# Moments and scaling of the second sequence's tiles beside value matmuls, and softmax totals spread through DRAM instead of through the array

## The chip, the core and the metric

The kernel runs on one core of one Trainium2 chip. The metric is the device time of one execution in microseconds; lower is better. Besides the times there is one profiled execution, whose trace holds every engine's instructions with their begin and end.

## What is computed

The input is `x` with 4 sequences of 1024 rows and 1024 columns, all in fp32. First comes attention, then a top-1 mixture of small adapters, each with a residual:

```python
x = x + attn(layernorm(x), wq, wk, wv, wo)     # 32 heads of 32, rotary q and k, causal softmax
x = x + ffn(layernorm(x), route_w, A, Bw)      # 8 experts of rank 16, the best one by logit
# attn: probs = softmax(scores); out = probs @ v; out @ wo
```

The softmax is computed without its division: exponentials go into the value product, and the product is then multiplied by the reciprocals of the rows' totals.

## The kernel before, in words

**Tiling.** Four heads fill 128 partitions, so a sequence has 8 groups and the program has 32 *units* `(b, g)`, numbered `u` = 0 to 31. A unit projects q, k and v of the next unit (six chains of eight 128x128x512 matmuls, lines 337 and 385), computes its own scores (L430) round by round, and multiplies exponentials by values (L626). The 1024 queries of a unit are two *blocks* of 512; block 1 of unit `u` is finished early in unit `u+1`.

**Order.** All instructions are written out in one order; each engine runs its own in that order, and semaphores join them. `SLOTS` lists the eleven rounds of a unit: score rounds, with "second" (apply block 1 of the unit before) and "first" (apply block 0 of this unit) among them. Between rounds, `fill` takes *steps* from a queue `todo`: projections of the next unit, and from the second sequence on also the output projection (L743) and the adapter stage (L765, L804) of a tile of the sequence before, whose weights are streamed as chunks (L700). `postponed` holds small pieces of work that are let go after so many steps' cost.

**One round.** The scores land in the one PSUM tile `s` (pool `ps_s`, one buffer). ACT copies them to `pr` (L441), POOL adds the causal mask (L444), DVE finds each row's maximum (L462, L483), ACT takes exponentials and their row sums (L491), DVE transposes them in 32x32 squares (L516). `apply` then runs the value matmuls in two pieces, into the same PSUM tile `s`; between the pieces it calls `meanwhile`, which transposes the next values (L1087). `scale_values` (L646, two DVE instructions of 128x256) multiplies the product by the totals' reciprocals `by`, and only then is the PSUM tile free for the next score round.

**The reciprocals.** `join_sums` adds the row sums (L559) and takes the reciprocal (L560) as soon as a block's transposes are out. The reciprocals stand one per query row, and `by` needs them along the free axis, repeated over the 32 rows of each head. There are two ways:

- *By turning* (before: all of the first sequence, 16 blocks). POOL spreads them to `by` (L563); `spread_sums` transposes `by` with four 128x128 matmuls against the identity (L597), and ACT copies the result back (L598).
- *By DRAM* (before: the other three sequences, 48 blocks). DVE transposes them (L570, `recT`); `put` writes them to DRAM in four transfers (L576), `get` reads them back with each row repeated over 32 partitions, in four transfers (L581). All eight are issued by SP, whose queue also carries every other transfer of the kernel, in the written order. `put` waits for `recT`, `get` for `put` to land.

**The next sequence's input.** Class `Norm` holds it. `load` fetches a 128-row tile of `x`; `find` computes mean and variance on DVE (two L178, then L180, L182) and the reciprocal root on POOL (L184); `scale` applies them on DVE (L189); `turn` transposes the tile on the array. For the second sequence, tiles 0 to 5 are loaded, found and scaled by steps put into the queue of units 1, 2, 3, 4 and twice 5; tiles 6 and 7 have their own places in unit 6 (`own` steps), and the turning is done in units 6 and 7.

Of the kernel before, what the change touches and what calls it, by code (L numbers as in the profile page):

```python
# [71 lines left out]
def tile_preln_attn_then_top1_lora(  # L72
# [24 lines left out]
    NG = HEADS // HG  # L97
# [112 lines left out]
    units = [(b, g) for b in range(B) for g in range(NG)]  # L210
# [335 lines left out]

    bys = {}

    def join_sums(u, blk):

        if (u, blk) in bys or any((u, t) in places for t in range(blk * QT, (blk + 1) * QT)):
            return
        den = dens.pop((u, blk)).rearrange("p (t c) h -> p c h t", c=2)
        rec = rec_sb[:, blk, : HG * TB].rearrange("p (h t) -> p h t", t=TB)
        for i in range(P // SQ):
            rows, other = slice(i * SQ, (i + 1) * SQ), slice((i ^ 1) * SQ, ((i ^ 1) + 1) * SQ)
            nc.vector.tensor_tensor(rec[rows], den[rows, i % 2], den[other, i % 2], ALU.add)  # L559
        nc.vector.reciprocal(rec_sb[:, blk, : HG * TB], rec_sb[:, blk, : HG * TB])  # L560
        if units[u][0] == 0:
            by = big.tile([P, TB, P], F32, tag="by", name=f"by_{u}_{blk}")
            nc.gpsimd.tensor_copy(  # L563
                by.rearrange("p t (h d) -> p t h d", d=HD),
                rec.rearrange("p h t -> p t h").unsqueeze(3).to_broadcast([P, TB, HG, HD]),
            )
            bys[u, blk] = by, None
            return
        turned = small.tile([P, SQ], F32, tag="recT", name=f"recT_{u}_{blk}", bufs=2)
        nc.vector.transpose(turned, rec_sb[:, blk])  # L570
        there = dram.tile([HG * TB, P // SQ, SQ], F32, tag="recs", name=f"recs_{u}_{blk}")
        by = big.tile([P, TB * P], F32, tag="by", name=f"by_{u}_{blk}")

        def put():
            for i in range(P // SQ):
                nc.sync.dma_start(there[:, i], turned[i * SQ : i * SQ + HG * TB])  # L576

        def get():
            for h in range(HG):
                of_h = there[h * TB : (h + 1) * TB]  # L580
                nc.sync.dma_start(  # L581
                    by[h * HD : (h + 1) * HD],
                    bass.AP(of_h.tensor, of_h.offset, [[0, HD], [1, TB * P]]),
                )

        left = [put, get]
        bys[u, blk] = by, left
        for cost in (2.0, 5.0):
            postponed.append([cost, lambda: left and left.pop(0)()])
# [279 lines left out]
    def behind(steps, at, step):  # L869

        steps.insert(steps.index(at) + 1, step)

    norms = {}
    between, late_fetch = [], {}
    tail = []
    for u, (b, g) in enumerate(units):
        project, new_tail = [], []
        if b:
            fetch, (project,), new_tail = finish_steps(
                b - 1, g, "resident" if u == len(units) - 1 else "stream"  # L880
            )
            if g:
                apart = 3 if g + 1 == NG and u + 1 < len(units) else 8
                between[-1].insert(max(0, len(between[-1]) - apart), fetch)
            else:
                late_fetch[u] = fetch

        if u + 1 < len(units) and g + 1 == NG:  # L890
            last_v = between[-1]
            if b:
                norm = Norm(b + 1, {0: (2,), 2: (5,), 3: (6,)}, {3: "q", 4: "k", 6: "q"})
                load = [Step(lambda norm=norm, t=t: norm.load(t), 0.0) for t in range(2)]
                for at, step in (
                    (own["k", 0][0], load[0]),
                    (own["v", 0][0], norm.finding(0)),
                    (own["v", 0][1], load[1]),
                    (own["v", 0][2], norm.scaling(0)),
                    (own["v", 0][4], norm.finding(1)),  # L900
                    (own["v", 0][6], norm.turning(0)),
                    (own["v", 0][7], norm.scaling(1)),
                    (own["k", 1][2], norm.finding(2)),
                    (own["k", 1][3], norm.turning(1)),
                    (own["k", 1][5], norm.scaling(2)),
                ):
                    behind(last_v, at, step)
            else:

                norm = Norm(b + 1, {0: (7,)}, {5: "chunk", 6: "chunk"})  # L910
                for t, (unit, at) in enumerate(((1, 24), (2, 24), (3, 24), (4, 24), (5, 12), (5, 36))):
                    steps = between[unit]
                    for k, step in enumerate((norm.load, norm.find, norm.scale)):
                        steps.insert(at - 8 + 5 * k, Step(lambda step=step, t=t: step(t), 0.0))
                for at, step in (
                    (own["q", 0][0], Step(lambda norm=norm: norm.load(6), 0.0)),
                    (own["q", 1][0], norm.finding(6)),
                    (own["q", 1][3], norm.scaling(6)),
                    (own["v", 1][5], norm.finding(7)),
                    (own["v", 1][7], norm.scaling(7)),  # L920
                ):
                    behind(last_v, at, step)
                for t, at in enumerate((("k", 1), ("k", 1), ("k", 1), ("v", 1))):
                    behind(last_v, own[at][(1 + 3 * t) % NC], norm.turning(t))
            steps = change_steps(u + 1, norm, project, tail, held)
            norms[b + 1] = norm
        else:
            steps = []
            held = []
            if u + 1 < len(units):  # L930


                ends = g + 2 == NG and b + 1 < B
                own = {}
                for n, tb in ENDING if ends else USUAL:
                    own[n, tb] = chain(u + 1, n, tb)
                    if ends and b and (n, tb) == ("v", 1):
                        held = own[n, tb]
                    else:
                        steps += own[n, tb]  # L940
            if not steps:
                steps = list(project)
            elif b and not g:
                steps = steps[:36] + weave(steps[36:], project)
            else:
                steps = weave(steps[:-6], project) + steps[-6:]
            if u + 1 == len(units):
                new_tail6 = tail
            n = len(steps)
            for k, s in reversed(list(enumerate(tail))):  # L950
                steps.insert(6 + k * n // 7, s)
        between.append(steps)
        tail = new_tail
# [110 lines left out]
    second, first_ = SLOTS.index("second"), SLOTS.index("first")  # L1064
    final = len(units) - 1
    for u, (b, g) in enumerate(units):
# [10 lines left out]
        for r, pieces in enumerate(SLOTS):  # L1077
            if pieces == "second":
                release_exps()
            if pieces == "second":  # L1080
# [4 lines left out]

                def meanwhile():
                    nc.vector.transpose(vTs[u], vTs[u])  # L1087

                if u:
                    apply(u - 1, 1, meanwhile)  # L1090
# [3 lines left out]
            elif pieces == "first":  # L1094
                apply(u, 0)
                find_tops(u)
                ended.clear()
            else:
                release_exps()
                turn_probabilities()  # L1100
                if second < r < first_:
                    join_sums(u, 0)
                score_round(u, pieces)
                if r == second - 1 and u:
                    while any((u - 1, t) in places for t in range(QT, 2 * QT)):
                        exponentiate_some(1)
                        turn_probabilities()
                    join_sums(u - 1, 1)
                if r != first_ - 1:
                    find_tops(u)  # L1110
                exponentiate_some(SHARE / 3)
                next_exp.extend((u, t, h) for t in ended for h in range(HG))
                if r != first_ - 1:
                    ended.clear()
                if r in (second + 1, first_ + 1):
                    for put in stores:
                        put()
                    stores.clear()
                    if u == final and r == first_ + 1:
                        load_adapter()  # L1120
                if r == second + 2:
                    scatter(loads, 2)
                    if u in late_fetch:
                        do(late_fetch[u])
                        for k in range(3 if b == 1 else 0):
                            load_chunk(k)
# [75 lines left out]
```

## Time and profile before

| what | value |
|---|---|
| time, median of 3 runs | 2752.6 us (2751.11 to 2756.06) |
| profiled execution: its own time | 2752.48 us |
| its span, first to last instruction | 2750.7 us |
| mean granted TensorE clock | 0.992 |
| a unit of the first sequence, V transpose to V transpose (L1087), units 1 to 5 | 68.3 to 72.1 us |
| a steady unit of the second sequence | 81.5 us |
| L597 four transposes of `by`: PE MATMUL x64 | 287 ns each by the record |
| L598 copy of `by` on ACT x16; L563 spread on POOL x16 | 581 ns; 612 ns |
| L570 `recT` on DVE x48 | 211 ns |
| L576, L581 issue on SP, x192 each | median 412 ns, 419 ns |
| L178 moments, L189 scaling of a tile (DVE) | 682 ns each of two; 1043 ns |

In the profile, PE is TensorE's matmuls, PEld its weight loads, DVE VectorE, ACT ScalarE, POOL GpSimd, SP the queue that issues transfers (SPq its instruction stream). A timeline row has its begin and length in us, the engine, the line, the operation, the tiles written and read, and how many alike follow each other; in brackets stands the idle time of the engine just ahead and what released it. One fp32 matmul stands in the records as two passes, so a chain of eight steps is 16 records.

### The profile page before, as it was taken

To read this page: it belongs to the slowest core of one execution; us is meant where nothing else is said; L and a number is where in the kernel's file an instruction comes from. 1 tells how busy PE (TensorE), PEld (TensorE's weight loads), DVE (VectorE), ACT (ScalarE), POOL (GpSimd) and SP (SyncE) were. 2 spreads that over 40 slices of the span, in tenths; PEclk is the share of its full clock that TensorE was granted. 3 is DMA by queue.
4 is the path that set the end of the run, shared out by engine and by line. 5 is a ranking of instruction groups with operands and counts; after the bars stand their busy time and mean duration, and the time that the engine had idled before them with its cause. 6 is when DMAs were issued, how large, how long until landed. Compare 5 with 4: busy or idle time off the path is not lost.

```text
span 2750.7 us, 84042 instructions
## 1 busy us (share of the span) xinstructions
PE 2680.1 (97%) x35136; PEld 1307.2 (48%) x35136; DVE 2143.1 (78%) x4249; ACT 1727.5 (63%) x4985; POOL 608.5 (22%) x852
## 2 busy tenths in 40 slices
PE   8999999999999999989999999998999999999998
PEld 5444444444445444444444454444544444444445
DVE  4888889887877877887777778787777777788555
ACT  2877777776666766666666666665576665666521
POOL 2222222222222222212222222221222221222000
PEclk9999999999999999999999999999999999999999
DMA  3222222225544455661655544565255555446421
GB/s 117 52 63 63 63 71 71 63 48 126 154 131 130 136 154 143 157 181 51 182 139 141 134 125 125 154 177 148 66 167 153 139 140 135 126 126 203 133 71 54
DMA packets 463659, 330.84 MB, mean 120 GB/s; under 512 B 159536, under 2 KB 380976, under 8 KB 463280
## 3 DMA queue, kind: packets, MB, share of 16 engines
q1 hardware_dynamic: 463280, 325.47, 43.5%
q8 instruction: 276, 4.52, 0.7%
q14 instruction: 103, 0.84, 0.1%
HBM read 275.17 MB, written 50.20 MB: 118 GB/s over the span
## 4 chain that ended last, share of the span: by engine, by line
PE 79%; DVE 13%; ACT 2%; DMA 2%; POOL 1%; issue 1%; SPq 1%; POOLq 0%; DVEq 0%; ACTq 0%
PE po L743 14%; PE pq L337 14%; PE pk L337 13%; PE pv L337 12%; PE s L430 11%; PE av L626 8%; DVE pr L516 4%; DVE top L462 4%; PE ph L765 2%; PE pf L804 2%; DMA chunk<-in_wo 1%; ACT pr L441 1%; DVE both L483 1%; PE pt_f L201 1%; ACT pr L491 1%
## 5 line engine op out<-in xcount | busy, mean ns | idle before, releaser
L491 ACT ACTIVATE pr<-pr,both 128x256 f32<-128x256 f32 (+15 forms) x2048 | 1044.5, 518 | 68.8 <-DVE both L483 68.8
L441 ACT COPY pr<-s 128x640 f32<-128x640 f32 (+14 forms) x544 | 525.3, 1017 | 678.8 <-PE s L430 678.1
L462 DVE TENSOR_REDUCE top<-pr 128x2 f32<-128x960 f32 (+15 forms) x768 | 650.8, 894 | 267.3 <-POOL pr L444 266.7
L516 DVE STREAM_TRANSPOSE pr<-pr 128x1024 f32<-128x1024 f32 (+11 forms) x768 | 664.4, 907 | 35.1 <-ACT pr L491 31.7
L444 POOL TENSOR_TENSOR pr<-pr,causal_sb 128x128 f32<-128x128 f32 x512 | 240.8, 477 | 1173.7 <-ACT pr L441 1165.4
L337 PE MATMUL pv<-xnT,wv 128*128 128x512 f32 x1024 | 488.7, 604 | 0.0
L337 PE MATMUL pq<-xnT,wq 128*128 128x512 f32 x1008 | 479.3, 603 | 0.2 <-ACT xnT L203 0.2
L337 PE MATMUL pk<-xnT,wk 128*128 128x512 f32 x1008 | 476.4, 602 | 0.0
L430 PE MATMUL s<-kT,qT 32*32 32x256 f32 (+4 forms) x17408 | 398.5, 390 | 21.1 <-DVE at L646 13.4
L491 ACT ACTIVATION_READ_ACCUMULATOR pr<-pr,both 128x1 f32 x2048 | 400.4, 195 | 0.0
L743 PE MATMUL po<-chunk,attn 128*128 128x512 f32 x736 | 383.7, 607 | 9.0 <-DMA chunk<-in_wo 8.6
L430 PEld LDWEIGHTS s<-kT,qT 32*32 32x32 f32 x17408 | 189.4, 103 | 280.4 <-issue 123.2
L337 PEld LDWEIGHTS pk<-xnT,wk 128*128 128x128 f32 x1008 | 181.2, 190 | 234.7 <-issue 234.3
L337 PEld LDWEIGHTS pv<-xnT,wv 128*128 128x128 f32 x1024 | 187.1, 191 | 220.2 <-issue 219.6
L337 PEld LDWEIGHTS pq<-xnT,wq 128*128 128x128 f32 x1008 | 183.9, 192 | 226.6 <-issue 224.8
L626 PE MATMUL av<-pr,vals 64*32 64x256 f32 (+3 forms) x12288 | 271.7, 319 | 7.4 <-DVE pr L516 6.8
L626 PEld LDWEIGHTS av<-pr,vals 64*32 64x32 f32 x12288 | 213.1, 106 | 116.6 <-issue 68.9
L483 DVE TENSOR_TENSOR both<-top 32x4 f32<-32x4 f32 (+3 forms) x1152 | 204.9, 178 | 23.8
L743 PEld LDWEIGHTS po<-chunk,attn 128*128 128x128 f32 x736 | 135.7, 191 | 178.0 <-issue 144.7
L646 DVE TENSOR_TENSOR at<-av,by 128x256 f32<-128x256 f32 x128 | 48.1, 417 | 123.6 <-PE av L626 79.6
L743 PE MATMUL po<-wo,attn 128*128 128x512 f32 x256 | 117.7, 601 | 0.0
L375 POOL TENSOR_TENSOR qT<-qT,swapq 128x512 f32<-128x512 f32 x64 | 81.7, 1277 | 146.3 <-DVE swapq L371 146.3
(89 smaller groups left out, 1575.7 us busy)
## 6 DMA issues: line engine op xcount, KB each, us to landing
chunk<-in_wo SPq DMA_DIRECT2D x368, 256.0 KB, 4.0
vals<-vd SPq DMA_DIRECT2D x256, 128.0 KB, 4.4
x<-in_x SPq DMA_DIRECT2D x56, 512.0 KB, 5.4
wq<-in_wq SPq DMA_DIRECT2D x32, 512.0 KB, 4.7
wk<-in_wk SPq DMA_DIRECT2D x32, 512.0 KB, 4.0
wv<-in_wv SPq DMA_DIRECT2D x32, 512.0 KB, 4.4
vd<-vT SPq DMA_DIRECT2D x128, 128.0 KB, 4.8
out_y<-x SPq DMA_DIRECT2D x32, 512.0 KB, 2.6
```

The lines of the kernel that those rows point to most:

```text
L337: nc.tensor.matmul(at["p"], lhsT=wt[:, c, :], rhs=xnTs[b, tb][:, c, :], start=(c == 0), stop=(c == NC - 1),)
L375: nc.gpsimd.tensor_tensor(dst[:, cols], dst[:, cols], other, ALU.add)
L430: nc.tensor.matmul(sc[i * SQ : (i + 1) * SQ, h, at : at + w].rearrange("p (j k) -> p j k", k=SQ), lhsT=of_q[rows, 2 * t + half], rhs=of_k[ ...
L441: nc.scalar.copy(pr[:, :, k0 : k0 + w], sc[:, :, at : at + w])
L444: nc.gpsimd.tensor_tensor(diagonal, diagonal, causal_sb.unsqueeze(1).to_broadcast([P, HG, SQ]), ALU.add)
L462: nc.vector.tensor_reduce(top[:, k, h : h + step], places[u, t][:, h : h + step, :], AX.X, ALU.max, negate=True,)
L483: nc.vector.tensor_tensor(dst[rows], src[rows], src[other], op)
L491: nc.scalar.activation(pr[:, h, :], pr[:, h, :], AF.Exp, bias=tops[u, t][:, h : h + 1], accum_out=dens[u, t // QT][:, t % QT, h : h + 1],)
L516: nc.vector.transpose(pr, pr)
L626: nc.tensor.matmul(avs[half][h * HD : (h + 1) * HD, t0:, :], lhsT=v[rows, j, h * HD : (h + 1) * HD], rhs=rhs, start=(j == 0), stop=(j == n ...
L743: nc.tensor.matmul(st["po"], lhsT=lhsT, rhs=rhs, start=(c == start), stop=(c == stop))
L765: nc.tensor.matmul(ph, lhsT=st["ynT"][:, c, :], rhs=w[:, c - i * RA, :], start=(c == 0), stop=(c == NC - 1),)
```

## The change

It has two parts. First, in the first sequence the totals go by DRAM too, and the turning is kept for blocks near a change of sequence: with `at = u + blk`, those with `at` 0, with `at % 8 == 7`, with `at` 32, and block 0 of unit 6. So 12 blocks of the first sequence (block 1 of units 0 to 5 and 7, block 0 of units 1 to 5) change from turning to DRAM, and 7 blocks of later sequences ((14,1), (15,0), (22,1), (23,0), (30,1), (31,0), (31,1)) change from DRAM to turning.

Second, tiles 0 to 5 of the second sequence are loaded by a step at the end of units 0 to 5; their moments are found in `meanwhile` of the following unit (between the two pieces of value matmuls of "second", behind the V transpose), and their scaling is put ahead of the score round that follows "second". Of the instructions that each engine is given, the order changes as follows. DVE has the moments between L1087 and L646 of block 1, and the scaling behind the transposes that follow L646, ahead of that round's maxima; before, both stood between the rounds of tiles 15 and 14. In unit 6 tile 5's and tile 6's moments and scalings both stand ahead of that L646. POOL has L184 ahead of the qT addition of L375 in place of behind it. SP has the eight transfers of a block just ahead of the store of that block's product (L659).

```diff
+    def by_turning(u, blk):
+        at = u + blk
+        return at == 0 or at % NG == NG - 1 or at >= len(units) or (u, blk) == (NG - 2, 0)
...
-        if units[u][0] == 0:
+        if by_turning(u, blk):
...
-                for t, (unit, at) in enumerate(((1, 24), (2, 24), (3, 24), (4, 24), (5, 12), (5, 36))):
-                    steps = between[unit]
-                    for k, step in enumerate((norm.load, norm.find, norm.scale)):
-                        steps.insert(at - 8 + 5 * k, Step(lambda step=step, t=t: step(t), 0.0))
+                for t in range(NG - 2):
+                    ahead_of[t + 1] = (
+                        lambda norm=norm, t=t: norm.find(t),
+                        lambda norm=norm, t=t: norm.scale(t),
+                    )
+                    between[t].append(Step(lambda norm=norm, t=t: norm.load(t), 0.0))
...
                 def meanwhile():
                     nc.vector.transpose(vTs[u], vTs[u])
+                    if u in ahead_of:
+                        ahead_of[u][0]()
...
                     join_sums(u, 0)
+                if r == second + 1 and u in ahead_of:
+                    ahead_of[u][1]()
                 score_round(u, pieces)
```

More of the change, by code (lines that the diff above doesn't have):

```diff
@@ L871, in behind @@
         steps.insert(steps.index(at) + 1, step)
-    norms = {}
+    norms, ahead_of = {}, {}
     between, late_fetch = [], {}
```

## The prediction, as put on record

> **What bounds the kernel now.** I read the page first: busy shares, then the chain that ended last.
>
> ```profile
> PE 2680.1 (97%) x35136; PEld 1307.2 (48%) x35136; DVE 2143.1 (78%) x4249; ACT 1727.5 (63%) x4985; POOL 608.5 (22%) x852
> PE 79%; DVE 13%; ACT 2%; DMA 2%; POOL 1%; issue 1%; SPq 1%; POOLq 0%; DVEq 0%; ACTq 0%
> ```
>
> PE bounds the whole, but DVE holds 13% of the chain. Where? The windows view, by stage (per engine: busy us and count; then the granted clock, DMA share and GB/s):
>
> ```profile
> 142.10:493.20 351.10, 332.54 (x5180) 157.06 (x5188) 302.49 (x592) 263.48 (x767) 97.20 (x138) 0.98 0.27 65
> 637.30:1123.50 486.20, 485.52 (x6492) 232.59 (x6491) 386.26 (x759) 315.58 (x921) 108.57 (x150) 1.00 0.52 140
> ```
>
> The second row is the second sequence: PE idles 0.7 us in 486. The first row is units 1 to 5 of the first sequence: PE idles 18.6 us in 351, the clock is 0.98, and DVE is busy 86%. PE's timeline of unit 2 shows a typical loss:
>
> ```profile
> 246.56 2.74 PE L337 MATMUL pv<-xnT,wv 128*128 128x512 f32 x6
> 252.01 1.61 PE L430 MATMUL s<-kT,qT 32*32 32x384 f32 x64 [2.71 <-DVE at L646]
> 253.55 4.36 PE L337 MATMUL pv<-xnT,wv 128*128 128x512 f32 x6
> ```
>
> The scores wait for L646 of block 0, which frees the PSUM tile. And DVE of the same unit:
>
> ```profile
> 214.51 0.75 DVE L646 TENSOR_TENSOR at<-av,by 128x256 f32<-128x256 f32 x2 [2.74 <-ACT by L598]
> ...
> 221.10 1.11 DVE L462 TENSOR_REDUCE top<-pr 128x4 f32<-128x384 f32 x3 [3.22 <-POOL pr L444]
> ...
> 231.38 1.29 DVE L178 BATCH_NORM_STATS2 st_a<-x 128x6 f32<-128x512 f32 x2
> ...
> 233.77 1.75 DVE L189 TENSOR_SCALAR x<-x,mv_a,rstd_a 128x1024 f32<-128x1024 f32 x1 [0.67 <-POOL rstd_a L184]
> ...
> 251.15 0.71 DVE L646 TENSOR_TENSOR at<-av,by 128x256 f32<-128x256 f32 x2
> ```
>
> DVE idles 2.74 and 3.22 us early in the unit, then runs almost without a break up to L646 of block 0 at 251.15, although its value matmuls ended at 246.07; POOL's mask (L444) costs another 1.20 us of waiting at 244.68. The norm work stands in that unbroken part: from 231.38 to 235.45 with its wait, 4.1 us.
>
> **Part 1: moments and scaling into DVE's idle time.** Moments (1.29 + 0.21 + 0.15, with gaps 1.7 us) go into the 2.74 us ahead of L646 of block 1; scaling (0.9 us in unit 6, 1.75 here where POOL works at the same time) goes into the 3.22 us. Both fit, so they cost nothing where they land. Without that cover they would delay the scores behind L646 one for one; the value matmuls end at 213.14, moments at about 213.5, L646 at 214.2, and PE needs the tile at 215.8: 1.6 us to spare. The new wait: L184 on POOL waits for the moments with the qT addition (L375) behind it, from 209.6 to about 213.5; that qT is read a unit later. SP's load of x (512 KB, 5.4 us to land) moves from inside the unit to the end of the one before, over 10 us ahead of the moments. In unit 6 two tiles' moments and scalings (2.6 us more) stand ahead of L646; it ends at about 498.6, and the scores want the tile at 498.7: no gain there, no loss.
>
> Then maxima of tile 14 move from 237.65 to about 233.6, and POOL's 1.20 us ahead of tile 13's go too (its L563 copy, 0.6 us, is gone from the queue). L646 of block 0 could start 5.2 us earlier by DVE; it starts when the value matmuls are done, and PE's 2.7 us go. What is late next is counted below.
>
> **What a gap costs beside itself.** The windows of the clock, around the same gap (PE busy, count, clock among the columns):
>
> ```profile
> 249.80:253.20 3.40, 1.19 (x62) 0.84 (x64) 3.40 (x6) 1.41 (x5) 0.55 (x1) 1.00 0.14 52
> 253.20:256.60 3.40, 3.40 (x30) 1.52 (x7) 3.40 (x4) 1.93 (x2) 0.46 (x1) 0.51 0.09 30
> 256.60:260.00 3.40, 3.40 (x69) 1.49 (x69) 3.29 (x8) 1.40 (x5) 0.00 (x0) 0.99 0.00 0
> ```
>
> Behind a window in which PE was busy 1.19 of 3.4 us, the next window has half the clock: six passes of pv took 4.29 us to the next instruction, 2.67 elsewhere. The Trainium skill, "TensorE: Matmul & The Clock Gate", Part 1 and the section on oscillation, says that the clock falls after a fully idle window of about 3.4 us, and to avoid gaps longer than that. By that rule no gap of 2.7 us costs any clock, and only the gaps count. The trace disagrees: five such windows stand in the stretch (181.6, 253.2, 335.2, 393.2, 461.4), each behind a gap of 1.7 to 2.8 us, each worth 3.4/2 = 1.7 us. The rule would give 8.5 us less gain; I take the trace.
>
> The sum for units 1 to 5: PE's gaps are 18.5 us. Of these 1.03 (219.3) and 1.19 (289.8) wait for nothing that is shown; I leave them: 16.3. Clock: 8.5.
>
> **Part 2: totals by DRAM in 12 blocks.** Removed per block: four transposes on PE (0.49 us from their start to the next instruction), 0.58 us on ACT, 0.61 us on POOL; added 0.21 us of DVE and eight issues on SP. Ten lie in units 1 to 5: 4.9 us of PE; the other two, (5,1) and (7,1), 1.0 us.
>
> Does `by` arrive in time? The nearest row is the same trip in the second sequence:
>
> ```profile
> 760.03 0.76 DVE L646 TENSOR_TENSOR at<-av,by 128x256 f32<-128x256 f32 x2 [2.22 <-DMA wq<-in_wq]
> ```
>
> There `recT` ended at 750.91 with its issue free at 750.94, and the landing was 6.2 us after it; in most blocks of the second sequence L646 starts 5.8 us behind recT, in 7 to 8 us with other transfers ahead. So L646 already waits for the trip there, without cost to PE. In the first sequence DVE has 6.55 us of work between recT and L646 of block 0 (maxima 2.1, joining 0.66, swap 1.43, transposes 2.36), and PE reaches the scores 2.0 us after that L646: the trip may take up to 8.6 us. Block 1 has over 9 us. DMA is 27% busy here. Ends: nothing, to 12 x 0.5 us if half the trips take 9 to 10; I take nothing. On SP, `get` waits about 1.1 us for `put`; behind it stands the store of the same block, which waits for L646 anyway, and the V store.
>
> **Part 3: turning where sequences meet.** Added: 7 x 0.49 = 3.4 us of PE. L646 comes about 1.2 us later (transposes, ACT); PE has 5 to 9 us of other matmuls before the next scores, so that is hidden; without it, 1.2 each. Removed: SP's stops at `put`. They show here:
>
> ```profile
> 1878.64 2.07 PE L743 MATMUL po<-chunk,attn 128*128 128x512 f32 x2 [3.11 <-DMA chunk<-in_wo]
> ```
>
> and in SP's queue:
>
> ```profile
> 1873.16 2.69 SPq L576 DMA_DIRECT2D recs<-recT  x4
> 1875.95 1.32 SPq L700 DMA_DIRECT2D chunk<-in_wo  x3
> ```
>
> SP stood at `put` from 1867.6 to 1875.9; the chunks behind it landed too late. Without it, PE's next stop is the hidden vector's transpose, which waits for DVE until 1877.3 in place of 1880.5: 3.2 us, plus 2.0 us from the half clock that followed to 1884.8. The same place in the first change of sequence (1206.62) lost 1.03 us. Gain 6.2. At (30,1), (31,0) and (31,1) I see no gain.
>
> **Sum.** 16.3 + 8.5 + 4.9 + 1.0 + 6.2 - 3.4 = 33.5. Against it: what is late next. Units 1 to 5 at 351.1 - 29.7 = 321.4 are 64.3 each; DVE has 60.5 busy in each, 0.4 more with recT, and about 2 us of waits for POOL's masks remain: 63. From L646 of block 0 to the last transposes that the next value matmuls need, DVE runs unbroken 23 us (251.9 to 274.9), and PE's matmuls between take 23.1. That is even. I count 0.5 us per unit, 2.5 in all. So 31 us: against the profiled execution's own 2752.48 (span 2750.7 and 1.8 around it, within 0.2 of the median) 2721.5.
>
> **The rivals.**
> *DVE becomes the bound.* Unit 0 speaks for it: no norm work, no gap at L646, and yet PE waited 2.61 us for pr (L516) at 135.09; the unit took 66.4. Against it: there DVE had 24.9 us behind L646, by another order of transposes, and started 1.4 us late by ACT. At 66.4 each, units 1 to 5 save 19.1, all together 22.9: 2730. If those waits halve the clock again, 2738.
> *The trip is late* (the slower end). Place: L646 of block 0. From 8.6 us on each us stops PE, and costs half a clock window. At 13 us, as one trip took at 2550.7 behind loads of x, 12 blocks lose 4.4 + 1.7 each: 73 against 33, about 2792. Against it: nothing stands between put and get on SP here, and DMA is 27% busy.
> *The moments don't hide:* x not landed, or the DVE idle already eaten. Then L646 of block 1 moves and each unit loses what part 1 wins: 5 x 4.4 less, 2744. The early load speaks against it.
> *More than counted:* the unexplained 2.2 us and the later chunk gap (1.79 at 1898.25 with its clock) go too: 2712.
>
> **Chances.** As forecast 0.54 (2714 to 2728); more 0.08; DVE the bound 0.26; moments not hidden 0.05; trip late 0.07, of which 0.05 slower. A measurement tells 0.2% (5.5 us) from no change. Faster 0.92, within 0.03, slower 0.05. The range 2709 to 2739 leaves out under 0.2.
>
> **What would show it.** Right: PE's waits "s <- at L646" and "at <- by L598" gone from the first sequence, clock near 1.00 from 142 to 470, units of 64 to 65 us, chunk wait after (22,1) gone. Wrong: L646 idle on a DMA in the first sequence with PE behind it, or av L626 waiting for pr L516 in each unit.

## The result, and the profile after

| | before | after | difference |
|---|---|---|---|
| median, first comparison (6 runs each) | 2750.94 us (2746.85 to 2756.06) | 2730.38 us (2726.64 to 2733.6) | -20.6 us; ratio 0.9925 [0.9911, 0.9938] |
| median, in a later set (27 and 6 runs) | 2750.49 | 2729.05 | -21.4 us; ratio 0.9925 [0.9907, 0.9943] |
| profiled execution, own time | 2752.48 | 2729.0 | -23.5 us |
| mean granted clock in it | 0.992 | 0.995 | |

Faster, as forecast, by two thirds of the 31 us that were forecast. The profiled execution of before is 1.5 us above the median of its six runs and that of after 1.4 below, so the two profiles side by side show 2.9 us more than the medians do. Two executions of one kernel can differ by several us in one stage; where single profiles are compared below, 2 or 3 us are not told from chance.

The page of the kernel after: engines, the chain that ended last, and the group of the score matmuls with the idle time ahead of it.

```profile
PE 2671.2 (98%) x35116; PEld 1305.0 (48%) x35116; DVE 2141.2 (79%) x4254; ACT 1725.2 (63%) x4980; POOL 604.4 (22%) x847
PE 79%; DVE 13%; ACT 3%; DMA 2%; POOL 1%; issue 1%; SPq 0%; POOLq 0%; DVEq 0%; ACTq 0%
L430 PE MATMUL s<-kT,qT 32*32 32x256 f32 (+4 forms) x17408 | 393.8, 385 | 8.7 <-POOL pr L444 3.3
```

The same group on the page of before:

```profile
L430 PE MATMUL s<-kT,qT 32*32 32x256 f32 (+4 forms) x17408 | 398.5, 390 | 21.1 <-DVE at L646 13.4
```

The scores' waits fell from 21.1 to 8.7 us, and those for L646 (L652 in the new file: lines from 549 to 910 are shifted by 6) are no longer their largest part. DVE still holds 13% of the chain: its share tells nothing of the 20 us.

Where it went, by stage: I take the moments at which PE begins the value matmuls of a block, and how far the profile of after stands ahead of before there. At block 1 of unit 0 it is 0.45 us behind; at block 1 of unit 5, 23.7 ahead (units 1 to 5: 24.2 us won); three units on, 22.9 (0.8 lost); behind the first meeting of sequences (the place where one sequence ends and the next begins), 22.3; at unit 17, 21.5; behind the second meeting, 27.8; up to (30,1), 28.0; at the end, 23.45. So units 1 to 5 carry it, the second meeting adds 6, the end gives 4.6 back.

Units 1 to 5 in the windows view, from one such moment to the other, before and then after (columns as in the prediction):

```profile
135.10:486.50 351.40, 332.84 (x5164) 156.99 (x5164) 302.70 (x593) 263.09 (x767) 97.33 (x137) 0.98 0.27 65
```

```profile
135.50:462.80 327.30, 322.26 (x5126) 149.94 (x5126) 299.42 (x598) 257.81 (x758) 90.20 (x126) 0.99 0.31 76
```

PE idles 5.0 us in place of 18.6, and its own work takes 10.6 us less: half clocks and transposes. DVE's own work fell by 3.3 us. From one such moment to the next, the five units took 66.3, 64.1, 64.0, 65.2 and 67.7 us, 65.5 in the mean, against 70.3 before. PE's timeline of unit 2 (the place that the prediction showed at 252.01):

```profile
241.25 2.84 PE L337 MATMUL pv<-xnT,wv 128*128 128x512 f32 x6
244.03 1.49 PE L430 MATMUL s<-kT,qT 32*32 32x384 f32 x64
...
253.98 1.43 PE L430 MATMUL s<-kT,qT 32*32 32x256 f32 x64 [0.63 <-POOL pr L444]
```

The wait of 2.71 us is gone, a small one for POOL's mask has come two rounds later. And DVE's timeline of that unit:

```profile
209.29 1.25 DVE L178 BATCH_NORM_STATS2 st_a<-x 128x6 f32<-128x512 f32 x2
210.57 0.21 DVE L180 BATCH_NORM_AGGREGATE mv_a<-st_a 128x2 f32<-128x12 f32 x1
210.81 0.15 DVE L182 TENSOR_SCALAR ve_a<-mv_a 128x1 f32<-128x1 f32 x1
211.02 0.76 DVE L652 TENSOR_TENSOR at<-av,by 128x256 f32<-128x256 f32 x2
...
214.30 0.77 DVE L189 TENSOR_SCALAR x<-x,mv_a,rstd_a 128x1024 f32<-128x1024 f32 x1
...
242.01 0.71 DVE L652 TENSOR_TENSOR at<-av,by 128x256 f32<-128x256 f32 x2
```

The moments stand where DVE idled 2.74 us, and L652 follows without a wait. L652 of block 0 starts 0.76 us behind the end of its value matmuls (241.25); before, 5.1 us. No L652 of the changed blocks in units 1 to 5 idles on a transfer in this profile (one does in a second profile of the kernel, 0.33 us). And the scaling takes 0.77 us in place of 1.75, in units 1 to 4 alike: at its old place it ran beside GpSimd's product of q and the cosines (L370), at the new one GpSimd is idle. So about 1 us of the 4.1 was not hidden but went away.

What was given back shows at three places. Unit 6, PE's timeline (four half scalings took 2.82 us of DVE ahead of L652, one of them 1.49 beside GpSimd's L370; in the kernel with the norm work alone, below, the same four took 1.88 and nothing waits here):

```profile
476.12 2.02 PE L430 MATMUL s<-kT,qT 32*32 32x96 f32 x128 [0.97 <-DVE at L652]
```

The meetings of sequences and, in the last line, the last unit, again in PE's timeline:

```profile
1199.04 1.12 PE L749 MATMUL po<-chunk,attn 128*128 128x512 f32 x2 [1.31 <-DMA chunk<-in_wo]
1201.14 2.08 PE L749 MATMUL po<-chunk,attn 128*128 128x512 f32 x2 [0.98 <-DMA chunk<-in_wo]
...
1871.57 2.13 PE L749 MATMUL po<-chunk,attn 128*128 128x512 f32 x4 [1.47 <-DMA chunk<-in_wo]
...
2558.76 5.80 PE L749 MATMUL po<-wo,attn 128*128 128x512 f32 x9 [2.33 <-DMA attn<-attn]
```

The stop of 3.11 us at the second meeting is gone, but chunks are still late elsewhere in it and in the first. The last line is the last unit: a wait that the kernel before did not have. The load of that tile of attn was issued at 2551.06 and landed 7.6 us later; before, it took 4.7 us and landed just in time. A half clock followed both at 1200.9 and at 2559.4.

### The profile page after: what moved, and what is told of

It is laid out like the page before. It is cut to its first block, busy times and chain, and to the rows that moved or that the text cites. A ratio compares the mean times of both kernels' runs of the same rounds, so it can differ in the third digit from the quotient of the medians.

```text
span 2727.2 us, 84063 instructions
## 1 busy us (share of the span) xinstructions
PE 2671.2 (98%) x35116; PEld 1305.0 (48%) x35116; DVE 2141.2 (79%) x4254; ACT 1725.2 (63%) x4980; POOL 604.4 (22%) x847
## 4 chain that ended last, share of the span: by engine, by line
PE 79%; DVE 13%; ACT 3%; DMA 2%; POOL 1%; issue 1%; SPq 0%; POOLq 0%; DVEq 0%; ACTq 0%
PE po L749 15%; PE pq L337 14%; PE pk L337 13%; PE pv L337 11%; PE s L430 11%; PE av L632 8%; DVE top L462 4%; DVE pr L516 3%; PE ph L771 2%; PE pf L810 2%; ACT pr L491 1%; ACT pr L441 1%; DVE both L483 1%; PE pt_f L201 1%; DMA chunk<-in_wo 1%
## 5 line engine op out<-in xcount | busy, mean ns | idle before, releaser
L483 DVE TENSOR_TENSOR both<-top 32x4 f32<-32x4 f32 (+3 forms) x1152 | 206.6, 179 | 23.8
L652 DVE TENSOR_TENSOR at<-av,by 128x256 f32<-128x256 f32 x128 | 48.1, 417 | 110.0 <-PE av L632 71.5
L370 POOL TENSOR_TENSOR qT<-rawq,cos_sb 128x512 f32<-128x512 f32 x64 | 82.1, 1283 | 143.0 <-ACT rawq L363 143.0
```

What stands on the lines that cost most here:

```text
L370: nc.gpsimd.tensor_tensor(dst[:, cols], raw, cos_sb[:, cols], ALU.mult)
L483: nc.vector.tensor_tensor(dst[rows], src[rows], src[other], op)
```

## The experiments

Twelve kernels, in three sets; those of a set ran on one chip and share the runs of before (medians 2750.42, 2752.64 and 2750.49). The last column is from the profile, between the moments used above: length, and PE's idle time in it. In the cuts of code, "-" is a line of the changed kernel and "+" what stands in its place; "..." marks what is left out.

| kernel | median | against before | ratio [95%] | units 1 to 5: length, idle |
|---|---|---|---|---|
| before | | | | 351.4, 18.6 |
| norm work alone | 2728.95 | -21.5 | 0.9922 [0.9908, 0.9935] | 332.2, 6.1 |
| twelve blocks by DRAM alone | 2756.74 | +6.3 | 1.0024 [1.0015, 1.0032] | 355.9, 23.1 |
| turning at meetings and end alone | 2745.74 | -4.7 | 0.9985 [0.9976, 0.9994] | |
| norm work and twelve blocks | 2730.93 | -19.5 | 0.9928 [0.9916, 0.994] | 326.7, 4.5 |
| whole, end by DRAM | 2728.16 | -24.5 | 0.9911 [0.9897, 0.9924] | |
| norm work, turning at meetings | 2726.19 | -26.5 | 0.9901 [0.9886, 0.9917] | |
| whole, tile 6 later | 2726.17 | -26.5 | 0.9906 [0.9893, 0.992] | |
| moments moved, scaling left | 2733.16 | -19.5 | 0.9932 [0.992, 0.9945] | 337.4, 10.8 |
| whole, again | 2729.05 | -21.4 | 0.9925 [0.9907, 0.9943] | 327.3, 5.0 (first profile) |
| whole, tile 6 later, end by DRAM | 2724.69 | -25.8 | 0.9905 [0.9887, 0.9922] | |
| only block 1 by DRAM | 2749.1 | -1.4 | 1.0 [0.9988, 1.0012] | 346.6, 14.7 |
| useless matmuls in the gap | 2751.64 | +1.2 | 1.0001 [0.999, 1.0011] | 348.0, 6.2 |

### The parts alone

**The norm work alone.** The new loads, moments and scaling, with the rule for the totals as before:

```diff
-        return at == 0 or at % NG == NG - 1 or at >= len(units) or (u, blk) == (NG - 2, 0)
+        return units[u][0] == 0
```

> The norm work of tiles 0 to 5 moved as in the change, the totals by the two ways exactly as before. My theory (VectorE's order ahead of L646 of block 0 is the cause, and the array's four transposes only a price of 0.49 us): most of the 16.3 us of gaps and most of the 8.5 us of half clock go, the transposes stay: 17 to 22 us faster than before. In PE's timeline the 2.7 us waits for L646 in units 1 to 5 are gone or under 1 us. Rival 1 (the way of the totals carries the gain: GpSimd's copy, ScalarE's copy and the array's transposes hold L646 up): under 8 us faster, the waits for L646 stay above 1.5 us. Rival 2 (the moments don't hide while ScalarE copies by: L646 of block 1 moves back): 10 to 14 us, with a new wait of the scores behind L646 of block 1.

2728.95 us, 21.5 faster: all of the change's gain, in one of its parts. PE's timeline and DVE's, unit 2:

```profile
257.45 1.44 PE L430 MATMUL s<-kT,qT 32*32 32x256 f32 x64 [0.97 <-ACT pr L441]
```

```profile
212.13 0.76 DVE L652 TENSOR_TENSOR at<-av,by 128x256 f32<-128x256 f32 x2 [1.14 <-ACT by L604]
```

The wait for L652 of block 0 is gone although ACT and the array still turn the totals; L652 of block 1 still waits for ACT, behind the moments, and no score waits for that. Rivals 1 and 2 fall. In units 1 to 5 its profile won 19.2 us (351.4 to 332.2).

**Twelve blocks by DRAM alone.** The norm work where it was, the first sequence's part of the rule, nothing turned later:

```diff
+        return at == 0 or u < NG and at % NG == NG - 1 or (u, blk) == (NG - 2, 0)
```

> Twelve blocks of the first sequence by DRAM, no turning added later, the norm work where it was before. My theory: 5.9 us of transposes go; GpSimd's copy (0.6 us) no longer stands ahead of the masks, so L646 of block 0 comes some 1.2 us earlier and the gaps of 2.7 us shrink to about 1.5 and stay; half clocks behind them go in some units: 8 to 14 us faster. Rival 1 (the totals carry the gain): 17 us or more faster. Rival 2 (the trip to DRAM takes back what it saves): 0 to 5 us faster, with waits of L646 on a transfer in the first sequence.

2756.74 us, 6.3 slower; every theory expected a gain, so each of them was wrong here, mine by 14 us and more. L652 does wait on a transfer, as rival 2 said. PE's timeline and then DVE's, unit 2:

```profile
253.66 2.37 PE L430 MATMUL s<-kT,qT 32*32 32x384 f32 x64 [4.52 <-DVE at L652]
```

```profile
249.06 2.37 DVE L516 STREAM_TRANSPOSE pr<-pr 128x1024 f32<-128x1024 f32 x2
252.76 0.76 DVE L652 TENSOR_TENSOR at<-av,by 128x256 f32<-128x256 f32 x2 [1.33 <-DMA by<-recs]
```

The trip from the end of recT to by took 6.3 to 7.7 us for block 0 of units 1 to 5, and L652 of block 0 idled 0.8 to 1.3 us on it in four of the five: DVE, which sets the pace of these units, stood still where it had not. It is busy 8 us more in the stretch as well (2.3 for recT; the small sums, L565 and L483, took 6 us longer, for which I have no cause). The gap of 2.7 us became 4.0 to 4.5 in four units, with longer half clocks. In the whole change the same trips took 5.6 to 6.1 us behind block 0 and fit; why they were shorter there was not found.

**Only block 1 by DRAM**, block 0 of the first sequence turned as before:

```diff
+        return at == 0 or u < NG and (blk == 0 or at % NG == NG - 1)
```

> Norm work as before; of the first sequence only block 1 of units 0 to 5 and 7 goes by DRAM, block 0 is turned as before. All twelve blocks by DRAM were 6.3 us slower than before. Theory (the trip of block 0 ends behind VectorE's 6.4 us of other work, at the end of its unbroken part; block 1's ends where L646 waited for ScalarE before): only the 3.4 us of transposes go and L652 of block 1 idles no longer than before: 1 to 4 us faster. Rival (eight more transfers per block disturb others, whichever block it is): 2 to 5 us slower.

2749.1 us, no change that can be told; only its profile won 4.8 us in units 1 to 5. The two kernels differ in block 0 of units 1 to 5 alone, and the loss is gone with it, so it was theirs. The rival's 2 to 5 us slower is not seen, though the interval reaches 3.3. The 3.4 us of transposes are not surely won either.

**Norm work and twelve blocks**, nothing turned in later sequences (the rule of the kernel with twelve blocks alone, on the whole change):

> The norm work moved and twelve blocks of the first sequence by DRAM, nothing turned in later sequences. By my account of the traces units 1 to 8 give 23 us and the rest of the kernel stays: 22 to 24 us faster than before, 1 to 3 us slower or faster than the whole change. By the prediction's sum it would be 31 - 2.8, about 28 faster. If the first two parts don't add (each takes the same waits away), its gain is 5 us or more below the sum of the two kernels that do one part each.

2730.93 us, 19.5 faster: short of the 22 to 24, and within the intervals no different from the norm work alone. In units 1 to 5 its profile is 5.5 us shorter than that of the norm work alone (326.7 against 332.2): there the DRAM way pays as counted. It is lost behind them (part of it in unit 6, where this kernel too waits 0.96 us for L652): from block 1 of unit 5 to that of unit 8 it lost 2.4 us against before, where the norm work alone won 0.7, and by unit 17, over the first meeting, another 4.1, where the norm work alone lost 0.6.

**Turning at the meetings and the end alone**, first sequence and norm work as before:

```diff
+        return units[u][0] == 0 or at % NG == NG - 1 or at >= len(units)
```

> Turning added in the seven blocks of later sequences, the first sequence entirely as before. My prediction: 6.2 us of stops at put go, 3.4 us of transposes come: 2.8 us faster. My account of the two traces: the first meeting of sequences +0.5, the second -6.4, the third with the end +4.5 us: 1 to 2 us faster. Rival (the +4.5 us at the end come from the shift of everything before it, not from turning there): 5 us faster or more.

2745.74 us, 4.7 faster: more than the prediction's 2.8 and than my 1 to 2, and near the rival's 5. Its profile won 6.0 at the second meeting, lost 0.4 at the first and showed no late tile at the end, where its three turnings cost nothing (9.7 us ahead at (30,1), 9.65 at the end). It also stood 4.3 us ahead before the first meeting, where nothing is changed: so far can one execution differ from another in units 1 to 8.

### The sizes in dispute

**Moments moved, scaling left** between the rounds of tiles 14 and 13 (tile 5 as in the change; totals as before):

```diff
-                        lambda norm=norm, t=t: norm.scale(t),
+                        lambda norm=norm, t=t: norm.scale(t) if t + 3 == NG else None,
...
+                    if t + 3 < NG:
+                        between[t + 1].insert(26, Step(lambda norm=norm, t=t: norm.scale(t), 0.0))
```

> Of the norm work of tiles 0 to 4 only the load and the moments are moved (2.4 of 4.1 us of VectorE's time), the scaling (1.75 us) stays between the rounds of tiles 14 and 13; tile 5 as in the change; totals exactly as before, so to be compared with the kernel with only the norm work moved (-21.5). Theory of slack: VectorE waits 1.19 us for GpSimd's mask of tile 13 there, and the scores could wait 0.94 us more for L652, 2.1 us together; 1.75 us fit in, so nothing or little comes back: 18 to 21.5 us faster than before. Rival (the gain goes in proportion to the time taken out of the unbroken part): 12.5 us faster.

2733.16 us, 19.5 faster. But the scaling that was left is not the 1.75 us of the expectation. At this place GpSimd is idle, and DVE's timeline of unit 2 has

```profile
235.06 0.81 DVE L189 TENSOR_SCALAR x<-x,mv_a,rstd_a 128x1024 f32<-128x1024 f32 x1
```

So 3.3 of the 4.1 us had left the unbroken part, not 2.4. A gain in proportion to that would be 3.3/4.1 of 21.5, or 17.3 us (an estimate); the interval of this kernel reaches from 15 to 22 us. The rival's 12.5 falls with its premise, and the run does not tell a threshold from a proportion. What stayed did cost something: PE's wait in unit 2, 0.97 with the scaling moved, is

```profile
258.21 1.44 PE L430 MATMUL s<-kT,qT 32*32 32x256 f32 x64 [1.58 <-ACT pr L441]
```

There are 4.7 us more idle in units 1 to 5 (10.8 against 6.1), and the profile won 14.0 us there, against 19.2.

**Useless matmuls in the gap**, in the kernel before, ahead of the score round behind "first", in units 1 to 5:

```diff
+                if r == first_ + 1 and 0 < u < NG - 2:
+                    warm = bank([P, 512], f"warm_{u}")
+                    for _ in range(4):
+                        nc.tensor.matmul(warm, lhsT=eye_sb, rhs=cos_sb[:, :512], start=True, stop=True)
```

> The kernel before, with four useless 128x128x512 matmuls (1.85 us, into a bank that nobody reads) on TensorE just ahead of the score round that waits for L646 of block 0, in units 1 to 5. They fill most of the 2.7 us gap and move nothing else. The prediction's term of 8.5 us for the clock: five half windows go, 6 to 8.5 us faster although 9 us of work are added. Rival 1 (VectorE sets the pace of these units; what TensorE gains behind the gap it waits out at the next): the windows are full, and the time moves by less than 2 us. Rival 2 (the half clock has another cause): windows stay, 0 to 3 us slower.

2751.64 us: no change, rival 1. I had sized the matmuls wrongly: each stands in the trace as two passes, so four take 3.6 us, not 1.85, and they overran the gap by 0.65 us. PE's timeline, unit 2:

```profile
249.60 3.60 PE L1106 MATMUL warm<-cos_sb,eye_sb 128*128 128x512 f32 x8
253.13 1.49 PE L430 MATMUL s<-kT,qT 32*32 32x384 f32 x64
...
263.54 1.44 PE L430 MATMUL s<-kT,qT 32*32 32x256 f32 x64 [1.09 <-ACT pr L441]
```

The clock stays full from 14 to 540 us (in before five half windows stand there), and PE's real work in units 1 to 5 takes some 9 us less (341.8 less 5 x 3.6 is 323.8, against 332.8). None of it arrives: the round two later, which did not wait in unit 2 of before, now waits 1.09 us, and with the overrun of 0.65 that is the 1.7 us of the half window. The chain that ended last, in the profile of before, says why (start, length, engine, tile, line):

```profile
231.38 1.30 DVE st_a L178 x2
233.77 1.69 DVE x L189
...
251.86 4.13 DVE pr L516 x4
...
258.60 2.49 ACT pr L491 x7
261.11 1.90 ACT pr L441 x2
```

and then PE's timeline of before:

```profile
263.06 1.44 PE L430 MATMUL s<-kT,qT 32*32 32x256 f32 x64
```

The chain runs through the norm work, DVE's transposes and maxima, the exponentials and ACT's copy of the scores, and reaches PE at 263.06. The matmuls at half clock (253.55 to 257.84) are not on it: PE had done them, and was ready for this round, by the time the copy ended at 263.01. With the useless matmuls the copy ended at 263.49 and the round began at 263.54. In the other four units of before, that round already waited 0.3 to 1.7 us for the same copy. So DVE, and ACT behind it, set the pace here, and PE's faster clock is waited out.

**Tile 6 later.** Its moments and scaling behind L652 of block 1 in unit 6:

```diff
-                    (own["q", 1][0], norm.finding(6)),
-                    (own["q", 1][3], norm.scaling(6)),
+                    (own["k", 0][2], norm.finding(6)),
+                    (own["k", 0][5], norm.scaling(6)),
```

> The whole change, with moments and scaling of tile 6 moved behind L652 of block 1 in unit 6 and ahead of the maxima of tile 15. My account: the change lost 0.97 us of waiting there and about 0.6 us behind it, so 1 to 1.5 us faster than the whole change, 21.5 to 22.5 faster than before. Rival (tile 6 then stands in VectorE's unbroken part and makes L652 of block 0 late, as in before): the 2.7 us wait with a half clock comes to unit 6: 3 us slower than the whole change.

2726.17 us, 26.5 faster. PE and DVE in unit 6:

```profile
474.35 1.91 PE L430 MATMUL s<-kT,qT 32*32 32x96 f32 x128
```

```profile
470.84 0.76 DVE L652 TENSOR_TENSOR at<-av,by 128x256 f32<-128x256 f32 x2 [0.68 <-PE av L632]
```

21.5 to 22.5 were expected. The wait of 0.97 us is gone and L652 waits for its matmuls. From block 1 of unit 5 to that of unit 8 this kernel won 1.2 us on before (2.3 with the end by DRAM too). The kernels with tile 6 at the change's place lost 0.8 and 2.0 (two profiles of the change) and 0.2 (the change with the end by DRAM). So the place cost 1.4 to 4.3 us by these profiles, more than the wait itself; where the rest was lost was not followed. How much of the median's gain is this edit can't be told across sets.

**The end.** Blocks (30,1), (31,0) and (31,1) by DRAM as before:

```diff
-        return at == 0 or at % NG == NG - 1 or at >= len(units) or (u, blk) == (NG - 2, 0)
+        return at == 0 or at % NG == NG - 1 and at < len(units) - 1 or (u, blk) == (NG - 2, 0)
```

> The whole change, but blocks (30,1), (31,0) and (31,1) by DRAM as before. The profile of the whole change stood 28.0 us ahead of before at the last unit and 23.5 at the end, with a new wait of 2.33 us for the tile of attn at 2556 us and a half clock behind it. If turning at the end costs that: 24 to 26 us faster than before. Rival (the tile's load landed late, 7.6 us after its issue in place of 4.7, by the traffic of that moment, whatever is turned): 20 to 22 us faster, as the whole change.

2728.16 us, 24.5 faster, as expected of it if the turning costs; in its profile 28.4 us won at the last unit and 27.5 at the end. And **the whole change again**:

> The whole change, unchanged, beside the other kernels of this set on the same chip: 20 to 22 us faster than before. In three profiles with the end turned, two showed the wait of 2.2 to 2.3 us for the tile of attn in the last unit and one did not; five with the end by DRAM, none. If turning there causes it, it stands in this profile too; if it is the traffic of the moment, it is there or not by chance, and the tile's landing (4.7 to 9 us after its issue) decides.

2729.05 us, with the same wait in its profile, 2.2 us for the tile of attn. With the end turned, three of four profiles wait 2.2 to 2.3 us for that tile and one not at all; with the end by DRAM, before's among them, six of ten don't wait and four wait 0.6 to 1.2 us (the expectation's "none" overlooked such). So it leans on the turning, but not on it alone. None of the six kernels in which all of the first sequence is turned waits, the one with the end turned among them; of the eight profiles of kernels with blocks of the first sequence by DRAM, seven wait. So turning the end cost something only where the first sequence went by DRAM as well, and how that acts on a place so far behind it was not found. The order of transfers ahead of the load is the same in the one profile without the wait, where the load landed after 4.7 us, not 7.6. Why the load lands late stays open.

**The meetings**, with the norm work moved, all of the first sequence turned, the end by DRAM:

```diff
+        return units[u][0] == 0 or at % NG == NG - 1 and at < len(units) - 1
```

> The norm work moved, all of the first sequence turned as before, and (14,1), (15,0), (22,1), (23,0) turned where sequences meet; the end by DRAM. If the stops at put where sequences meet are a cost of their own, the two parts add: -21.5 by the norm work and -3 to -4.7 by the meetings, 24 to 26 us faster, better than every kernel so far. Rival (what is late at a meeting depends on how chunks, scores and the clock's windows happen to fall, and moves when the kernel is shifted): 20 to 22.5 us faster.

2726.19 us, 26.5 faster: the parts add, within their intervals (-21.5 and -4.7, the latter with the end turned, make -26.2). One profile of it won nothing at the second meeting, since a chunk was 2.76 us late and the clock fell for two windows: a single profile can't price a meeting, the medians can.

**The best of what was learnt**, the whole change with tile 6 later and the end by DRAM:

> The whole change with tile 6's moments and scaling behind L652 of block 1 in unit 6, and the last three blocks by DRAM: both losses of the change taken away at once. My account: 1.5 to 2.7 us for tile 6, 3 to 4 us for the end: 25 to 28 us faster than before, 4 to 6 faster than the whole change. Rival (each only shifts which stop comes at a meeting): 21 to 23.

2724.69 us (2721.63 to 2726.51), 25.8 faster than before and 4.4 than the whole change beside it on the same chip (2726.01 to 2735.13). It beats both the kernel before and the changed one; against the two kernels at 2726.2 the intervals overlap, and one of these, the norm work with turning at the meetings, leaves the DRAM way out of the first sequence entirely. Nor do the two losses add. By medians from different sets, moving tile 6 is worth 5.1 us with the end turned and 1.3 with the end by DRAM; taking the end by DRAM is worth 3.1 with tile 6 in the change's place, and nothing (-0.7) once tile 6 is moved.

## Why the prediction was right, and where its sum was off

**Faster, and by which mechanism: right.** DVE's order ahead of L646 of block 0 was the bound of units 1 to 5, and taking the 4.1 us of norm work out of it freed PE. The norm work alone shows it. The number was off: 2730.4 lies outside the 2714 to 2728 that had the greatest chance. It is what the rival "DVE becomes the bound" gave, 2730, but by luck. That rival put the loss at units of 66.4 us in which value matmuls wait for pr, and no value matmul waits for pr in units 1 to 5. The units took 65.5 in the mean, between its 66.4 and the 64.3 (64.8 with what is late next) of the forecast. The losses in unit 6 and at the end are in neither.

**Units 1 to 5: 27.2 us expected, 24.2 measured, each term a little short.** The two kernels split it. The norm work alone: idle 18.6 to 6.1, that is 12.5 where 16.3 less 2.5 was counted; PE's own work 332.8 to 326.1, 6.7 where the clock was put at 8.5. With twelve blocks by DRAM added: 3.9 of PE's work and 1.6 of idle, 5.5 where 4.9 was counted. The step "what is late next" named the wrong thing: not DVE's 23 us against PE's 23.1, but ACT's copy with the norm work alone (0.78 to 0.98 us in each unit) and POOL's mask in the whole change (0.62 to 0.77). Counted on the engine that sets the pace, the norm work alone comes out nearer: five times the 4.1 us taken from DVE are 20.5 us (an estimate), 19.2 were measured, and the prediction's terms make 22.3.

**That these terms are a sum was wrong.** Clock, transposes and gap were added as if each were lost by itself. Taken alone, the clock is worth nothing that can be told (useless matmuls: +1.2 us, with an interval from 2.8 faster to 3.0 slower), the twelve blocks cost 6.3 us, and the norm work is worth 21.5. The half windows were read rightly, and they did go; but they lay off the chain, so their 8.5 us was no gain of its own beside the gaps. The transposes paid 5.5 us in units 1 to 5 only once the norm work was away.

**The trip by DRAM at nothing: right in the changed kernel, not as a rule.** There it took 5.6 to 6.1 us behind block 0. Alone it took up to 7.7 and DVE idled. The rival's place, L646 of block 0, was right; its point of 8.6 us was reckoned from PE's need, where DVE's own 6.55 us decides as long as DVE sets the pace. In the first profile of the changed kernel 0.4 us of that or more were to spare; in the second, one L652 idled 0.33 us.

**Unit 6, "no gain there, no loss": wrong for the whole change**, which waits 0.97 us there and lost 0.8 to 2.0 us in units 6 to 8. With the norm work alone it held: the scores start without a wait. The step counted with the four transposes of (5,1) on PE, which part 2 takes away (0.5 us), and with scalings of half a us each, of which one took 1.49 beside GpSimd. The loss ate the 1.0 us of (5,1) and (7,1).

**Meetings.** 6.2 less four turnings, 2.0: 4.2 expected; 5.6 in the first profile of the change, about 1 in the second, about 5 by the medians of kernels with and without it (24.5 against 19.5, 26.5 against 21.5, from different sets). Right in size; the stop removed at the second came back in part as other chunk waits.

**The end.** Three turnings, 1.5 us, expected; 4.6 in the first profile: the tile of attn landed 7.6 us after its issue, 2.3 us of waiting and 1.7 of half clock. This wait was in no step; the turnings themselves cost nothing where they stood alone.

**The balance.** 31 expected, 20.6 measured. Between the two profiles 7.5 us are missing: 3.0 in units 1 to 5, 1.8 in units 6 to 8, 3.1 at the end, 1.0 of small differences elsewhere, less 1.4 at the meetings. The other 2.9 lie between profiles and medians: before's profiled execution is 1.5 us above its median, the other 1.4 below. I had taken 2752.48 for typical, since it lay within 0.2 of the median of three runs; 25, 9 and 27 later runs have 2750.4, 2752.6 and 2750.5. One sum of the rivals does not come out either: 2721.5 less the 2.2, the 1.8 and a half window's 1.7 is 2715.8, not 2712.

**The signs.** The waits for L646 are gone from units 1 to 5, but a new one stands in unit 6; the clock is full from 139 to 521 us, as named; of the five units, two lie above 65.2 us; the chunk wait of 3.11 us behind (22,1) is gone, and one of 1.47 stands in that meeting. Of the signs of being wrong none came in the first profile.

## What to carry to other kernels

Where two engines are nearly even, find the slower one and take work out of its unbroken part first: savings on the other engine, its clock included, are waited out until then, so their terms must not be added up one by one. The chain that ended last shows which of them count: a stretch at half clock that isn't on it is worth nothing yet. Price a wait from the engine that stands still in it, not only from the one at the end of the chain: a DRAM trip that TensorE never sees can still stop VectorE. Before work is called "left in place", read how long it takes in its new surroundings: the same scaling took 1.75 us beside GpSimd and 0.8 elsewhere. A change of 20 us made of parts is best run part by part; here one part carried all of it and another was a loss by itself.

## What the runs showed of the hardware

- **The clock.** In the 14 profiles of this study the clock fell to half 131 times, for one window of 3.41 us or two; in the window ahead, PE was idle for 46 to 100%. No window with over 59% idle was followed by full clock, and none under 46% by half; between 46 and 59% it went both ways (21 followed by half clock, 43 not). So somewhere around half a window of idling is enough. The windows lie on a fixed grid: in each profile all starts of half clock fit one spacing of 3.413 us within 0.001. So the same gap of 2.6 us at about 133 us halved the clock in 11 of the profiles and not in three; in one of the three, the kernel with the useless matmuls, its window was 56% idle and full clock followed. This is not the rule of a fully idle window that the prediction weighed.
- **Scaling beside GpSimd.** Of the 336 scalings of a full tile (L189, 128x1024) in the 14 profiles, the 232 with GpSimd idle took 0.76 to 0.82 us; the 76 that stood for 0.7 us or more beside GpSimd's product L370 took 0.93 to 1.77, in the median 1.75. The places were not varied one by one, so why is open.
- **Reads behind writes through DRAM were late more often on idle queues.** Over 325 trips of six profiles, the first read was issued about 1.5 us behind the issue of the last write in the usual case. It was 2.2 us or more in 58 of 162 trips where the DMA engines were under 5% busy in the 3 us ahead of the first write, but in 9 of 119 where they were 40 to 70% busy. The places differ in more than traffic, so the cause is open. The Trainium skill, "DMA: Bandwidth & Descriptors", the section on latency and other measured facts, says that lighter memory load makes the fixed cost smaller; these trips, sorted by how busy this core's DMA engines were and not by memory load, show no such thing.
